# Decoder layer on one core: the second norm's factors issued right behind the first norm's power on GpSimd, and the output bias added by VectorE in one operation per batch

## The chip, the core and the metric

The kernel runs on one core of a Trainium2 chip. A core has TensorE (PE in the profile, its weight loads PEld), VectorE (DVE), ScalarE (ACT), GpSimd (POOL) and SyncE (SP, which here only issues transfers). Each engine takes its instructions strictly in the order in which the program lists them. An instruction that waits for another engine holds up everything behind it in its own queue. The metric is the time on the device in microseconds for one execution, lower is better; several executions are timed and the median counts. One execution is also recorded by the profiler.

## The reference

One decoder layer in float32, on x of shape 16 x 256 x 256 (batch, token, width) and a context of 16 x 77 x 256. Three sublayers, each added to its input and followed by a norm without weights:

```
x = layernorm(x + recurrence(x))            # linear, causal convolution of 4, silu, 16 states scanned over tokens, linear
x = layernorm(x + cross_attention(ctx, x))  # 8 heads of 128
x = layernorm(x + experts(x))               # 8 experts, the best 2 of each token, a capacity of 512 tokens per expert

cross_attention:
  xn = layernorm(ctx) * gamma_media + beta_media
  ln = layernorm(x) * gamma_lat + beta_lat       # x has just been normed: it is normed a second time
  q = ln @ Wq + bq;   k, v = split(concat(xn, ln) @ Wkv + bkv)
  out = softmax(q k^T / sqrt(128)) v @ Wo + bo   # bo is the output's bias
```

The second norm of x in the cross attention needs no new statistics. If the first norm had variance v and factor r = (v + eps)^-0.5, the normed rows have mean 0 and variance v r^2, so the second factor is (v r^2 + eps)^-0.5.

## The kernel before, in words

The kernel goes through the 16 batches one after the other. The main part is one loop over 128 pairs of batch b and head h. For every head it issues keys and queries (`head_kq`, lines 609 and 614), scores and softmax (`head_softmax`, 624 to 634), the turned probabilities (`head_turn`, 646 to 649) and, two heads later, the product with the values (`head_out`, 660). A head costs TensorE some 6 us. Between the heads, lists called `steps`, `mid_steps` and `late_steps` put all other work at fixed places (b, h): the recurrence of later batches, the preparation of batch b+1, and the output projection, norm, routing and result of batch b-1.

The program is written as this sequence, and a scheduler then lists each engine's instructions by when it expects their inputs to be ready. So the order on an engine is not just the order of the source. `tc.issue_after(i)` keeps an instruction behind another one.

The places that matter here:

- `rec_out(nb)` norms the recurrence's result for batch nb. Statistics on VectorE (144 to 147), the power v^-0.5 on GpSimd (`ra`, line 136), and the normed rows `xs` on VectorE (151). It keeps the power's instruction as `normed[nb]`, and ends with the load of x for batch nb+2 (SP). For even nb it stands at head 1 of batch nb-1, for odd nb at head 3 of batch nb-2.
- `prep_norm(nb)` forms the factors of the second norm with `again`: `uz`, `u2z`, `u3z` and the power `rlz`, four small GpSimd operations in a chain (159, 161, 163, 136), and multiplies `xs` by them on VectorE into `zl` (522). For even nb it stands at head 2 of batch nb-1; for odd nb at head 0 of batch nb-1, about five heads after `rec_out`. TensorE then turns `zl` (534), VectorE writes `kvt` (536), and all keys, queries and values of batch nb come from that.
- `project_sums` and `project_pairs` (725 to 770) are the output projection of batch b-1 at heads 1 to 3 of batch b, in a form with fewer products: VectorE makes sums `osum` and differences `ot` of the heads' outputs in place (725, 726, then 729, 730), and TensorE multiplies them in two parts (750). The second part needs line 729.
- In part 0, `project_pairs` also makes `xb` = `xs` + bias on GpSimd, two operations of 128 x 256 per batch (743), issued after `normed[b + 2]` of the batch b that is projected. This holds for batches 0 to 13; batches 14 and 15 go through `project` and `norm_half` (692, 781). `xb` has one buffer, so the next batch's `xb` can be written only when line 151 has read the last one.
- `scatter_second` sends the second batch of a routed pair to the experts' rows in HBM: four indirect transfers issued by GpSimd (990), at head 1 of odd batches, also after `normed`.
- `settle(b)` forms the factors of the third norm's input in the same way (`uo` to `rlo`) and writes the result rows `o` on GpSimd (807).

Of the kernel before, what the change touches and what calls it, by code (L numbers as in the profile page):

```python
# [13 lines left out]
ALU = mybir.AluOpType  # L14
# [4 lines left out]
P = 128  # L19
B, S, D = 16, 256, 256  # L20
# [18 lines left out]
def decoder_layer(  # L39
# [29 lines left out]
    V, A, G, T = nc.vector, nc.scalar, nc.gpsimd, nc.tensor  # L69
# [14 lines left out]
    def bank(name, tag="mm", bufs=2):  # L84
        return ps.tile([P, 512], F32, tag=tag, bufs=bufs, name=name)
# [48 lines left out]
    def rsqrt(v, n, rows, name):  # L134
        r = small.tile([P, n], F32, tag="r", name=f"r{name}")
        powers.append(G.tensor_tensor(r[:rows], v[:rows], nhalf[:rows, 0:n], ALU.pow))
        return r

    def layernorm(dst, src, n, rows, name, behind=None):

        mv = small.tile([P, n, 2], F32, tag="mv", name=f"mv{name}")
        for i in range(n):
            st = small.tile([P, 6], F32, tag="st", name=f"st{name}_{i}")
            V.bn_stats(st[:rows], src[:rows, i, :])
            V.bn_aggr(mv[:rows, i, :], st[:rows])
        v = small.tile([P, n], F32, tag="v", name=f"v{name}")
        V.tensor_scalar(v[:rows], mv[:rows, :, 1], EPS, None, ALU.add)
        r = rsqrt(v, n, rows, name)
        for i in range(n):
            with tc.issue_after(behind.ins) if behind is not None else nullcontext():  # L150
                V.tensor_scalar(
                    dst[:rows, i, 0:D], src[:rows, i, :], mv[:rows, i, 0:1], r[:rows, i : i + 1], ALU.subtract, ALU.mult
                )
        return mv, r

    def again(mv, r, name):

        u = small.tile([P, 2], F32, tag="u", name=f"u{name}")
        G.tensor_tensor(u, mv[:, :, 1], r, ALU.mult)
        u2 = small.tile([P, 2], F32, tag="u2", name=f"u2{name}")  # L160
        G.tensor_tensor(u2, u, r, ALU.mult)
        u3 = small.tile([P, 2], F32, tag="u3", name=f"u3{name}")
        G.tensor_scalar(u3, u2, EPS, 1.0, ALU.add, ALU.mult)
        return rsqrt(u3, 2, P, f"l{name}")
# [15 lines left out]
    bo_s = wpool.tile([P, D], F32, tag="bo", name="bo_s")  # L180
# [24 lines left out]
    def load_x(b):  # L205
        xts[b] = aw.tile([P, 2, D], F32, tag="xt", bufs=3, name=f"xt{b}")
        nc.sync.dma_start(xts[b], x_in[b * S : (b + 1) * S, :].rearrange("(i p) d -> p i d", p=P))
# [116 lines left out]
    sums, yss, xs, stats = {}, {}, {}, {}  # L324
# [90 lines left out]
        for b, r in zip(members, rows):  # L415
            yss[b] = ys[r, :], outw[r, :]

    ysums, normed = {}, {}

    def rec_add(b, n):  # L420

# [12 lines left out]
    def rec_out(b):  # L434

        xs[b] = xpool.tile([P, 2, DX], F32, tag="xs", name=f"xs{b}")
        stats[b] = layernorm(xs[b], ysums.pop(b), 2, P, f"a{b}")
        normed[b] = powers[-1]
        if b + 2 < B:
            load_x(b + 2)  # L440
# [70 lines left out]

    def prep_norm(b):

        r2 = again(*stats.pop(b), f"z{b}")
        zl = b1.tile([P, 2, D], F32, tag="zl", name=f"zl{b}")
        for i in range(2):
            if turned is None:
                V.tensor_scalar(zl[:, i, :], xs[b][:, i, 0:D], r2[:, i : i + 1], None, ALU.mult)
                continue

            with tc.issue_after(turned.ins):
                V.tensor_scalar(zl[:, i, :], xs[b][:, i, 0:D], r2[:, i : i + 1], None, ALU.mult)
        zs[b] = zl
# [193 lines left out]
    def out_block(b, e, i):  # L717
        return outs_t[b].rearrange("p (g e) s -> p g e s", e=2)[:, :, e, i * P : (i + 1) * P]
# [13 lines left out]
    def project_pairs(b, part):  # L732


        x = lambda e, i: out_block(b, e, i)
        w = wo_block
        t = lambda i: wosum[:, i, :, :]
        if part == 0:
            pws[b] = bank(f"pw{b}")
            xbs[b] = xb = b1.tile([P, 2, D], F32, tag="xb", name=f"xb{b}")  # L740
            with tc.issue_after(normed[b + 2].ins):
                for j in range(2):
                    G.tensor_tensor(xb[:, j, :], xs[b][:, j, 0:D], bo_s, ALU.add)
            products = (0, x(0, 0), w(0, 0)), (1, osums[b], t(0)), (2, x(0, 1), w(0, 1))
        else:
            products = (3, x(0, 0), t(1)), (0, x(1, 0), w(1, 0)), (1, osums[b], w(1, 1)), (2, x(1, 1), t(2))
        p = pws[b]
        for r, lhsT, rhs in products:
            for g in range(H // 2):
                T.matmul(  # L750
                    p[:, r * P : (r + 1) * P],
                    lhsT=lhsT[:, g, :],
                    rhs=rhs[:, g, :],
                    start=(part == 0 and r == 0 and g == 0),
                    stop=(g == H // 2 - 1),
                    skip_group_check=True,
                )
        xb = xbs[b]
        y = xb.rearrange("p i d -> p (i d)")
        if part == 0:  # L760
            parts[b] = u = b1.tile([P, 3, P], F32, tag="u", name=f"u{b}")
            A.copy(u.rearrange("p r d -> p (r d)"), p[:, 0 : 3 * P])
            for r in (1, 2):
                V.tensor_tensor(y[:, 3 * P :], y[:, 3 * P :], u[:, r, :], ALU.add)
            return
        u = parts.pop(b)
        V.tensor_tensor(u[:, 0, :], u[:, 0, :], p[:, 3 * P :], ALU.add)
        V.tensor_tensor(y[:, 0 : 3 * P], y[:, 0 : 3 * P], p[:, 0 : 3 * P], ALU.add)
        y3 = y[:, P:].rearrange("p (r d) -> p r d", d=P)
        V.tensor_tensor(y3, y3, u[:, 0:1, :].broadcast_to([P, 3, P]), ALU.add)  # L770
        norms[b] = layernorm(xs[b], xb, 2, P, f"b{b}")
# [249 lines left out]
    for b in range(B):  # L1021
        nb = b + 1
        new_pair = nb % PB == 0 and nb < B
        if b > 0:
            early = 2 * int(b == B - 1)
            if b < B - 1:
                behind(b, 1, project_sums, b - 1, 0)
                at(b, 2, project_pairs, b - 1, 0)
                behind(b, 2, project_sums, b - 1, 1)
                at(b, 3, project_pairs, b - 1, 1)  # L1030
            else:
                at(b, 0, project_last)
                at(b, 2, project, b - 1, 0)
                at(b, 2, project, b - 1, 1)
            at(b, 5 - early, turn_tokens, b - 1)
            if b == B - 1:
                at(b, 6 - early, score_experts, b - 1)
                at(b, 6 - early, choose, b - 1, 1)
                at(b, 7 - early, dispatch, b - 1, 1)
            elif b % 2 == 0:  # L1040
                at(b, 6, score_pair, b - 2)
                behind(b, 6, turn_logits, b - 2)
                behind(b, 6, choose, b - 2, 2)
                behind(b, 7, dispatch, b - 2, 2)
            if b % 2 == 1 and 2 < b < B - 1:
                behind(b, 1, scatter_second, b - 3)
            at(b, 7, settle, b - 1)
        if new_pair:
# [3 lines left out]
            elif nb % 4 == 0:  # L1052
                at(b, 0, rec_state, nb, nb + 3)
                amid(b, 0, rec_scan, nb)
            at(b, 1, rec_add, nb, PB)
            at(b, 1, rec_out, nb)
            at(b, 2, prep_norm, nb)
            at(b, 3, rec_out, nb + 1)
            at(b, 3, prep_keys, nb)
            at(b, 3, prep_sums, nb)  # L1060
# [3 lines left out]
        elif b == 0:  # L1064
            for h in range(2):
                at(0, h, rec_in, 0, 2 * h, 1)
                at(0, h, rec_in, 0, 2 * h + 1, 1)
            at(0, 2, load_xT, 1)
            at(0, 2, rec_state, 1, 1)
            amid(0, 2, rec_scan, 1)  # L1070
            at(0, 3, rec_add, 1, 1)
            at(0, 3, rec_out, 1)
            at(0, 4, prep_norm, 1)
            at(0, 4, prep_keys, 1)
            at(0, 4, prep_sums, 1)
            for n, h in enumerate((5, 6, 7)):
                at(0, h, prep_values, 1, n, False)
                behind(0, h, prep_values, 1, n, True)
            for h in range(NCT - FIRST_CTX):
                behind(0, h, context, FIRST_CTX + h, False)  # L1080
        elif nb < B:
            at(b, 0, prep_norm, nb)
            at(b, 0, prep_keys, nb)
            at(b, 0, prep_sums, nb)
            for n, h in enumerate((1, 4, 6)):
                at(b, h, prep_values, nb, n, False)
                behind(b, h, prep_values, nb, n, True)
# [378 lines left out]
```

## Time and profile before

| what | value |
|---|---|
| time, median of 3 runs | 1169.77 us (1169.11 to 1172.89) |
| the profiled execution's own time | 1171.0 us |
| its span, first to last instruction | 1169.3 us |
| granted TensorE clock | 0.997 |
| busy PE / PEld / DVE / ACT / POOL | 97% / 70% / 67% / 43% / 27% |
| GpSimd, line 743 (`xb`) | 28 operations, 19.2 us |
| GpSimd, line 990 (scatters) | 64 transfers, 66.1 us |
| GpSimd, lines 159 to 163 and 136 for `rlz` | 16 times four operations, 22.0 us |

The share of an engine's busy time is an average over the whole span. The heads run from about 55 us to 1020 us; before that lie the first norms and loads, after it the experts. A matmul's end is modelled, so the lost time of TensorE is best read from the distance of starts: four `pq` matmuls in a row are normally followed by the next group 0.86 to 0.87 us after their first start, and eight `pw` matmuls 0.89 us after. What a wait costs is what lies above that.

### The profile page before, as it was taken

What the parts mean: (1) busy time and instruction counts of PE and PEld (TensorE: products, weight loads), DVE (VectorE), ACT (ScalarE), POOL (GpSimd) and SP (SyncE); (2) the same over time, 40 slices, a digit from 0 to 9 for tenths busy, and PEclk for the clock granted to TensorE, in tenths of its full rate; (3) what the DMA queues carried; (4) which work ended last, traced back from release to release, by engine and by line L of the source; (5) the groups of instructions that cost most, each with busy time, mean ns of one, the idle gap of its engine ahead of it and who ended that gap; (6) DMA issues with size and microseconds to landing.
All of it is one profiled execution on the core that took longest, in us unless ns stands there. A gap on an engine that the chain in (4) does not pass through costs nothing. (4 is left out here: it accounts for less than half of the span.)

```text
span 1169.3 us, 16020 instructions
## 1 busy us (share of the span) xinstructions
PE 1135.1 (97%) x5380; PEld 821.0 (70%) x5380; DVE 782.1 (67%) x2144; ACT 499.0 (43%) x1315; POOL 316.1 (27%) x565
## 2 busy tenths in 40 slices
PE   7999999999999999999999999999999999999996
PEld 3465676767787777677777777777777778876664
DVE  6655877676657776777567757865567555665666
ACT  3344444453444344444444444444444444523331
POOL 2201241114210530242015302340142014144455
PEclk9999999999999999999999999999999999999998
DMA  8741010001000110010000100000001000046652
GB/s 276 206 128 39 20 38 18 11 28 58 19 12 10 54 36 12 28 40 19 12 10 27 37 11 10 18 19 12 10 17 46 20 10 15 21 159 138 181 160 90
DMA packets 47417, 60.63 MB, mean 52 GB/s; under 512 B 7957, under 2 KB 37374, under 8 KB 47336
## 3 DMA queue, kind: packets, MB, share of 16 engines
q1 hardware_dynamic: 39686, 50.18, 14.1%
q0 software_dynamic: 6048, 9.22, 3.3%
q8 instruction: 42, 0.69, 0.2%
q10 hardware_dynamic: 1602, 0.23, 0.1%
q14 instruction: 39, 0.32, 0.1%
HBM read 36.33 MB, written 30.78 MB: 57 GB/s over the span
## 5 line engine op out<-in xcount | busy, mean ns | idle before, releaser
L660 PE MATMUL po<-ptt,v 128*128 128x256 f32 (+1 forms) x768 | 189.2, 381 | 1.6 <-DVE rs L632 1.6
L660 PEld LDWEIGHTS po<-ptt,v 128*128 128x128 f32 (+1 forms) x768 | 142.0, 190 | 51.7 <-issue 34.4
L609 PE MATMUL pk<-kvt,wkv_s 128*128 128x333 f32 x512 | 165.4, 444 | 0.0
L624 PE MATMUL s<-kt,qt 128*128 128x333 f32 x512 | 164.5, 443 | 0.0
L626 DVE TENSOR_REDUCE nm<-s 128x2 f32<-128x666 f32 x128 | 108.3, 846 | 72.1 <-PE s L624 68.1
L630 ACT ACTIVATE p<-s,nm 128x333 f32<-128x333 f32 x256 | 135.7, 536 | 44.5 <-DVE nm L626 44.2
L614 PE MATMUL pq<-kvt,wq_s 128*128 128x256 f32 x512 | 131.2, 378 | 0.0
L609 PEld LDWEIGHTS pk<-kvt,wkv_s 128*128 128x128 f32 x512 | 91.1, 191 | 45.6 <-issue 22.9
L668 ACT ACTIVATE ot<-po,bkv_s 128x256 f32<-128x256 f32 x128 | 60.9, 476 | 140.3 <-PE po L660 135.7
L624 PEld LDWEIGHTS s<-kt,qt 128*128 128x128 f32 x512 | 96.3, 188 | 31.6 <-issue 1.3
L614 PEld LDWEIGHTS pq<-kvt,wq_s 128*128 128x128 f32 x512 | 96.7, 189 | 30.8 <-issue 1.0
L649 ACT COPY ptt<-pb 77x256 f32<-77x256 f32 x128 | 47.3, 369 | 164.1 <-PE pb L646 161.0
L634 DVE TENSOR_SCALAR p<-p,rs 128x333 f32<-128x333 f32 x256 | 98.5, 421 | 3.3
L990 POOL DMA_INDIRECT xg<-xs,sidx x64 | 66.1, 1032 | 98.3 <-ACT ot L668 38.9
L648 DVE COPY ptt<-pa 128x512 f32<-128x512 f32 x128 | 87.3, 682 | 0.7 <-PE pa L646 0.7
L646 PEld LDWEIGHTS pa<-ident,p 128*128 128x128 f32 x512 | 63.9, 141 | 29.3
L611 ACT ACTIVATE kt<-pk,bkv_s 128x333 f32<-128x333 f32 x128 | 69.1, 540 | 28.2 <-PE pk L609 21.7
L646 PE MATMUL pa<-ident,p 128*128 128x128 f32 x512 | 76.8, 273 | 0.0
L351 DVE SCALAR_TENSOR_TENSOR cv<-hp,cw,cv 128x512 f32<-128x512 f32 (+1 forms) x108 | 74.1, 692 | 1.6
L616 ACT ACTIVATE qt<-pq,bqs 128x256 f32<-128x256 f32 x128 | 61.1, 478 | 20.2 <-PE pq L614 15.3
L336 PE MATMUL ph<-xT,inw 128*128 128x512 f32 (+1 forms) x144 | 63.1, 567 | 5.5 <-DMA inw<-in_in_wT 4.4
L1275 PE MATMUL pf<-w,it 128*128 128x256 f32 x272 | 61.3, 381 | 2.0 <-ACT ye L1285 1.7
(264 smaller groups left out, 1764.6 us busy)
## 6 DMA issues: line engine op xcount, KB each, us to landing
v<-vc SPq DMA_DIRECT2D x16, 308.0 KB
xg<-zero SPq DMA_DIRECT2D x34, 131.0 KB
xe<-xg SPq DMA_DIRECT2D x8, 524.0 KB
xt<-in_x_in SPq DMA_DIRECT2D x16, 256.0 KB
out<-o SPq DMA_DIRECT2D x16, 256.0 KB
w<-in_w1T SPq DMA_DIRECT2D x8, 512.0 KB
w<-in_w2T SPq DMA_DIRECT2D x8, 512.0 KB
oe<-ye SPq DMA_DIRECT2D x15, 256.0 KB
```

Source lines behind the costliest of these rows:

```text
L351: conv = V.scalar_tensor_tensor(cv, hp[:, :, k : k + S], cw[:, c, k : k + 1], cv, ALU.mult, ALU.add)
L609: T.matmul(pk[:, 0:J], lhsT=wkv_s[:, k, f], rhs=kvt[:, k, :], start=(k == 0), stop=(k == DC - 1))
L611: A.activation(kt, pk[:, 0:J], AF.Identity, bias=bkv_s[:, h : h + 1])
L614: T.matmul(pq[:, 0:S], lhsT=wq_s[:, k, f], rhs=kvt[:, k, 0:S], start=(k == 0), stop=(k == DC - 1))
L624: T.matmul(s[:, ic, 0:J], lhsT=qt[:, ic * P : (ic + 1) * P], rhs=kt, start=True, stop=True)
L626: V.tensor_reduce(nm, s[:, :, 0:J], AX.X, ALU.max, negate=True)
L630: A.activation(p[:, ic, :], s[:, ic, 0:J], AF.Exp, bias=nm[:, ic : ic + 1], accum_out=sm[:, ic : ic + 1])
L634: V.tensor_scalar(p[:, ic, :], p[:, ic, :], rs[:, ic : ic + 1], None, ALU.mult)
L646: T.transpose(dst[0:jn, c0 : c0 + P], pn[:, ic, j0 : j0 + jn], ident)
L648: turned = V.tensor_copy(ptt[:, 0:2, :], pt01.rearrange("p (j i) -> p j i", j=2))
L660: T.matmul(po[:, 0:S], lhsT=vs[b][0:jn, jc, h * DH : (h + 1) * DH], rhs=ptt[0:jn, jc, :], start=(jc == 0), stop=(jc == 2),)
L990: dma = G.indirect_dma_start(out=xg[:, :], out_offset=bass.IndirectOffsetOnAxis(ap=sidx[:, t, c : c + 1], axis=0), in_=xs[b + t // GT][:, ...
```

## The change

The factors of the second norm are formed in `rec_out`, right behind the norm's power, and kept in `factors` until `prep_norm` fetches them. The power that `normed` names becomes the last power issued, which is now `rlz` and no longer `ra`: what is issued after `normed` is issued behind the factors too. The bias is added to `xs` by one VectorE operation of 128 x 512 per batch, with the bias row read twice through a broadcast, and without `issue_after`.

```
-    ysums, normed = {}, {}
+    ysums, normed, factors = {}, {}, {}
 ...
         xs[b] = xpool.tile([P, 2, DX], F32, tag="xs", name=f"xs{b}")
         stats[b] = layernorm(xs[b], ysums.pop(b), 2, P, f"a{b}")
+
+        factors[b] = again(*stats[b], f"z{b}")
         normed[b] = powers[-1]
         if b + 2 < B:
             load_x(b + 2)
 ...
     def prep_norm(b):
 
-        r2 = again(*stats.pop(b), f"z{b}")
+        r2 = factors.pop(b)
         zl = b1.tile([P, 2, D], F32, tag="zl", name=f"zl{b}")
 ...
             xbs[b] = xb = b1.tile([P, 2, D], F32, tag="xb", name=f"xb{b}")
-            with tc.issue_after(normed[b + 2].ins):
-                for j in range(2):
-                    G.tensor_tensor(xb[:, j, :], xs[b][:, j, 0:D], bo_s, ALU.add)
+            V.tensor_tensor(xb, xs[b][:, :, 0:D], bo_s.unsqueeze(1).broadcast_to([P, 2, D]), ALU.add)
```

## The prediction, before the result was known

> **What bounds the kernel now.** I read the totals first, then the waits of TensorE and of VectorE, then the order of time around the longest of them.
>
> ```profile
> PE 1135.1 (97%) x5380; PEld 821.0 (70%) x5380; DVE 782.1 (67%) x2144; ACT 499.0 (43%) x1315; POOL 316.1 (27%) x565
> PE pw L750 <- DVE ot L729: 3.5, 6, 1.3
> ...
> DVE zl L522 <- POOL rlz L136: 31.7, 6, 5.3
> ```
>
> TensorE is the bound: of 1169.3 us only 34 are idle, and much of that lies in the first 55 us and in the experts' stage after 1020. So VectorE's 31.7 us of waiting for `rlz` are not 31.7 us to be had. They count only where TensorE ends up waiting: six times for `ot`, line 729, which stands behind `zl` on VectorE. One of the six in the order of time, GpSimd, then VectorE, then TensorE (start, length, operation; in brackets the idle time before and what ended it):
>
> ```profile
> 393.16 0.72 POOL L136 TENSOR_TENSOR ra<-va,nhalf 128x2 f32<-128x2 f32 x1 [0.67 <-DVE va L147]
> 394.07 1.18 POOL L990 DMA_INDIRECT xg<-xs,sidx  x1 [0.19 <-issue]
> ...
> 399.27 1.33 POOL L743 TENSOR_TENSOR xb<-xs,bo_s 128x256 f32<-128x256 f32 x2
> 400.55 0.20 POOL L159 TENSOR_TENSOR uz<-mva,ra 128x2 f32<-128x2 f32 x1
> ...
> 401.39 0.72 POOL L136 TENSOR_TENSOR rlz<-u3z,nhalf 128x2 f32<-128x2 f32 x1
> ```
>
> ```profile
> 395.96 0.90 DVE L634 TENSOR_SCALAR p<-p,rs 128x333 f32<-128x333 f32 x2
> 402.14 0.61 DVE L522 TENSOR_SCALAR zl<-xs,rlz 128x256 f32<-128x256 f32 x2 [5.29 <-POOL rlz L136]
> 402.68 0.68 DVE L729 TENSOR_TENSOR ot<-osum,ot 128x512 f32<-128x512 f32 x1
> ```
>
> ```profile
> 401.10 1.02 PE L614 MATMUL pq<-kvt,wq_s 128*128 128x256 f32 x4
> 403.41 1.16 PE L750 MATMUL pw<-wosum,ot 128*128 128x128 f32 x8 [1.29 <-DVE ot L729]
> ```
>
> `ra` ends at 393.88. Four scatters and two `xb` stand between it and the four small operations that end in `rlz` at 402.11. VectorE waits 5.29 us, TensorE loses 403.41 - 401.10 - 0.86 (the usual distance) = 1.45 us, and 0.11 more in the first group after the gap (1.00 us to the next start, normally 0.89).
>
> **The change part by part.** I set the built order of the changed kernel against the old one. TensorE's order is the same, so its time changes only by its waits.
>
> 1. *`rlz` ahead of the scatters and without `xb` between (batches 4, 6, 8, 10, 12, 14).* From 393.88 four operations at the pace of 400.55 to 402.11 take 1.56 us, so `rlz` is ready at 395.5, perhaps 1 us later beside VectorE. The new VectorE order has half of `zl` ahead of `p` and half behind; `p` starts at 395.96 anyhow. `ot` of line 729 then ends near 398.5, and TensorE wants it at 401.96. All six waits go: 3.5 us idle, and with the modelled ends (1.56 lost against 1.29 idle) 0.27 more each: 3.5 + 6 x 0.27 = 5.1 us. Gain 5.1. It cannot be a loss here: 3.4 us are left. What is late next is line 726 at the same places (TensorE's wait for it, 0.6 us at 395.90), which stands ahead of all this and stays. The scatters move back by 1.6 us; their rows are first read after 1010 us, so 0. On GpSimd only `tsum`, first needed at 408, stands behind them; 395.5 + 4 x 1.3 = 400.7, so 0.
>
> 2. *`xb` off GpSimd.* It frees 28 x 0.70 = 19.2 us there, which bounds nothing. But VectorE is slowed beside it: two `xs` take 1.46 us beside `xb`, against 0.74 elsewhere.
>
> ```profile
> 143.34 1.46 DVE L151 TENSOR_SCALAR xs<-xt,mva,ra 128x256 f32<-128x256 f32 x2 [0.83 <-POOL ra L136]
> ...
> 166.40 1.30 DVE L151 TENSOR_SCALAR xs<-xt,mva,ra 128x256 f32<-128x256 f32 x2 [0.60 <-POOL ra L136]
> ...
> 170.90 1.53 PE L660 MATMUL po<-ptt,v 128*128 128x256 f32 x6 [1.63 <-DVE rs L632]
> ```
>
> Behind the first, in an unbroken VectorE row, line 726 keeps TensorE idle for 0.69 us at 149.98; 0.72 earlier it does so hardly at all: gain 0.7. Behind the second come `cv` (1.12 instead of 0.75), `nm`, `cv` and the copy `ptt`, for which TensorE waits 1.63 us at 170.90: 0.56 + 0.37 = 0.9 us earlier. Gain together 1.6; below, 0 if the small GpSimd operations now beside them slow them as much. In later odd stages (413.62, 1.30 us) TensorE does not wait, so 0.
>
> 3. *`xb` on VectorE, 14 operations.* The nearest row is the sum of two SBUF tensors of the same shape in line 726: 0.68 us, 0.61 from start to start. Built places: batch 0 right before a 1.64 us wait for ScalarE (116.97), free. Odd batches (413) behind `rs`: the 0.56 that `xs` no longer loses pays for it. Batches 4, 8, 12 (350) behind `rs`: `p` would end at 352.6 and is wanted at 354.32, free. Left are batches 2, 6 and 10. There the new order has `xb` and one more `cv` ahead of `nm` and `ptt`:
>
> ```profile
> 471.40 0.75 DVE L351 SCALAR_TENSOR_TENSOR cv<-hp,cw,cv 128x512 f32<-128x512 f32 x1
> 472.06 0.85 DVE L626 TENSOR_REDUCE nm<-s 128x2 f32<-128x666 f32 x1
> 472.82 0.75 DVE L351 SCALAR_TENSOR_TENSOR cv<-hp,cw,cv 128x512 f32<-128x512 f32 x1
> 473.48 0.69 DVE L648 COPY ptt<-pa 128x512 f32<-128x512 f32 x1
> ...
> 474.80 1.46 PE L660 MATMUL po<-ptt,v 128*128 128x256 f32 x6
> ```
>
> `ptt` ends at 474.17; 0.61 (`xb`) and 0.66 (`cv`) later is 475.44, and TensorE wants it at 474.80: it waits 0.7 us. ScalarE's order changes there too (`kt` ahead of the exponentials, `qt` behind the tanh); `qt` is then ready near 476.5, and the scores that need it have moved to 476.8, so no second wait. Cost 3 x 0.7 = 2.1. Bounds: 0 if the scheduler's order costs nothing after all, 3 x (0.7 + 0.86) = 4.7 if each `xb` is slowed as `osum` is once (1.54 us at 391.46 beside GpSimd's `sums`, 0.68 without). I take 2.1, since at 472 GpSimd has only a power of two elements at work, beside which `cv` and `osum` at 146 us kept their 0.7.
>
> The Trainium skill speaks against this part: "SBUF — State Buffer", section "Who interferes with whom", says that a VectorE sum with both inputs in SBUF contends with a GpSimd operation that reads SBUF, the later one being blocked for the whole instruction. By that rule `osum` at 391.46 waits for `sums`, which ends at 392.45, and the trace agrees. For the three places the rule would make it the 4.7 above if GpSimd were ahead, 2.1 if not.
>
> 4. *Moves with one answer.* In batch 0 `rc8` now stands behind `u3z` and `rlz` (0.28 + 0.75 later); `ctx` needs it and TensorE waits there already (88.97): about 0.2 us lost. On SP the load of x for batch nb+2 goes ahead of a result's store and `w1` of expert 0 ahead of another; each is ready at about the same time as what it passes, 0. In odd batches the third norm's factors stand behind `rlz` instead of between two `xb`, same length, 0.
>
> Sum: -5.1 - 1.6 + 2.1 + 0.2 = **-4.4 us**. The profiled execution, 1171.0 us (span 1169.3 and 1.7 around it), would take 1166.6. It is 1.2 above the median, so for the median 1169.77 - 4.4 = **1165.4 us**, 0.38% faster.
>
> **The rivals.**
>
> *A, `xb` costs nothing on TensorE.* If at batches 2, 6, 10 the copy still comes in time: -6.5, 1163.3 us. For it: 10 of 14 places hide it. Against: 0.63 us of room for 1.27.
>
> *B, the shared reading of SBUF.* Each of the three places costs 1.56, and the small GpSimd chain takes half of the 1.6 back: -5.1 - 0.8 + 4.7 + 0.2 = -1.0, 1168.8 us. For it: `osum` at 391.46. Against: GpSimd is nearly idle at these places.
>
> *C, nothing moves.* TensorE's wait for line 729 stays under another releaser, for instance `p`, whose exponential is late. Then -1.6 + 2.1 + 0.2 = +0.7, 1170.5 us. Against: 3.4 us of room.
>
> *D, slower: VectorE's added work passes to TensorE at all 14 places.* Its place is between `rs` and `p`, its price 0.61 to 1.47 each. At 0.61 it is 8.5 + 0.2 - 6.7 = +2.0, 1171.8 us; blocked, at 1.47, it is 20.6 + 0.2 - 6.7 = +14.1, 1183.9 us. It is slower by over 0.3% from (6.5 + 3.5) / 14 = 0.71 each. For it: VectorE waits only 1 to 2 us per head. Against: the room counted in step 3.
>
> **How the numbers follow.** About 0.3% (3.5 us) is what a measurement can tell from no change; the three runs lie 3.8 us apart. Chances: the forecast 0.50, A 0.14, B 0.20, C 0.07, D 0.09 (within 0.3% at its lower price 0.02, slower 0.07). The forecast lies only 0.9 us beyond the bound, so of its 0.50 I count 0.43 as faster and 0.07 as within. Faster: 0.43 + 0.14 = 0.57. Within: 0.07 + 0.20 + 0.07 + 0.02 = 0.36. Slower: 0.07. The range goes from A less 0.8 for the spread, 1162.5, to B, rounded up, 1169.2; it leaves out C, D and a little of the ends, some 0.2.
>
> **What would show it.** Right: VectorE's wait for `rlz` falls from 31.7 us to under 5, TensorE's wait for line 729 to near 0; `xb` is a VectorE row of 14 at about 0.69 us; three new waits of TensorE before `po` for `ptt`, half a microsecond each, near 234, 474 and 714; GpSimd is 19 us less busy. Wrong: `xb` at over 1 us (B), waits for `ptt` or `p` in odd batches too (D), waits for 729 left (C).

## The result, and the profile after

| | kernel before | changed kernel |
|---|---|---|
| median, 12 executions each | 1171.57 us (1169.11 to 1173.54) | 1168.02 us (1164.15 to 1169.99) |
| profiled execution, own time | 1171.0 us | 1169.99 us |
| its span | 1169.3 us | 1168.3 us |
| heads, first `pk` to first `pe` | 967.94 us | 964.29 us |

The ratio is 0.9968 with a 95% interval of 0.9959 to 0.9977: 3.7 us faster, between 2.7 and 4.8. The kernel before, measured beside it, took 1171.57 us over 12 executions, where the first three had given 1169.77; against that new base the forecast of -4.4 us reads 1167.2. The forecast time itself, 1165.4, was missed by 2.6 us, of which 1.8 are the base. By the bare time of 1168.0 rival B's 1168.8 lies nearer than the forecast, so the ratio and the traces have to tell the two apart. The 3.7 us are also only just more than the 3.5 that the prediction set as the bound to no change.

The totals and the longest waits of TensorE and VectorE in the changed kernel (the lines of the source have moved by two, so the old 729 is now 731):

```profile
PE 1135.5 (97%) x5380; PEld 821.7 (70%) x5380; DVE 784.2 (67%) x2158; ACT 499.1 (43%) x1315; POOL 300.6 (26%) x537
PE po L662 <- DVE rs L634: 2.6, 4, 0.7
PE px L373 <- DMA xpw<-in_xp_wT: 2.0, 1, 2.0
...
PE pw L750 <- DVE ot L728: 1.2, 2, 0.6
```

```profile
DVE nm L628 <- PE s L626: 72.7, 55, 2.0
DVE u L767 <- PE pw L750: 41.4, 14, 3.2
```

VectorE's 31.7 us of waiting for `rlz` are gone altogether. More than half of them have turned into waits for TensorE's products (`u` behind `pw`, 22.4 us before and 41.4 now), which hold up nothing on TensorE. TensorE's six waits for line 729 are gone, and four waits before `po` stand in the list, three of them new.

The place that the prediction showed around 400 us, in the changed kernel, in the order of time on GpSimd, VectorE and TensorE:

```profile
393.86 0.72 POOL L136 TENSOR_TENSOR ra<-va,nhalf 128x2 f32<-128x2 f32 x1 [0.66 <-DVE va L147]
394.66 0.19 POOL L159 TENSOR_TENSOR uz<-mva,ra 128x2 f32<-128x2 f32 x1
...
395.49 0.69 POOL L136 TENSOR_TENSOR rlz<-u3z,nhalf 128x2 f32<-128x2 f32 x1
396.35 1.12 POOL L990 DMA_INDIRECT xg<-xs,sidx  x1 [0.17 <-issue]
```

```profile
396.54 0.34 DVE L524 TENSOR_SCALAR zl<-xs,rlz 128x256 f32<-128x256 f32 x1
396.79 0.84 DVE L636 TENSOR_SCALAR p<-p,rs 128x333 f32<-128x333 f32 x2
397.55 0.33 DVE L524 TENSOR_SCALAR zl<-xs,rlz 128x256 f32<-128x256 f32 x1
397.80 0.70 DVE L731 TENSOR_TENSOR ot<-osum,ot 128x512 f32<-128x512 f32 x1
```

```profile
401.80 1.02 PE L616 MATMUL pq<-kvt,wq_s 128*128 128x256 f32 x4
402.67 1.05 PE L750 MATMUL pw<-wosum,ot 128*128 128x128 f32 x8
```

`rlz` ends at 396.18, 1.6 us behind `ra`, with the scatters behind it. `ot` ends at 398.50 and is wanted at 402.67, so 4.2 us of room have taken the place of a wait of 1.29. The distance from `pq` to `pw` is the usual 0.87 us.

The price of the change, around 472 us (VectorE, then TensorE):

```profile
471.20 0.69 DVE L743 TENSOR_TENSOR xb<-xs,bo_s 128x512 f32<-128x512 f32 x1
471.81 0.75 DVE L351 SCALAR_TENSOR_TENSOR cv<-hp,cw,cv 128x512 f32<-128x512 f32 x1
472.47 0.85 DVE L628 TENSOR_REDUCE nm<-s 128x2 f32<-128x666 f32 x1
473.23 0.79 DVE L351 SCALAR_TENSOR_TENSOR cv<-hp,cw,cv 128x512 f32<-128x512 f32 x1
473.94 0.68 DVE L650 COPY ptt<-pa 128x512 f32<-128x512 f32 x1
```

```profile
473.09 1.02 PE L576 MATMUL pv<-wsum,tsum 128*128 128x512 f32 x2
474.77 1.53 PE L662 MATMUL po<-ptt,v 128*128 128x256 f32 x6 [0.66 <-DVE rs L634]
```

`xb` and one more `cv` stand ahead of the copy `ptt`, which ends at 474.62; `po` starts 0.15 us later. (The profile names `rs`, which is ready at about the same time. `po` reads `ptt`, and with the bias added twice, below, where `rs` starts only 1 us after `po`, the profile names `ptt` for the same wait of 0.66 us.)

TensorE runs the same 5380 matmuls in the same order in both kernels, so one can take, for each matmul, its start after minus its start before. Where that difference steps, time was won or lost. All steps between 50 and 1010 us, each with the refill of up to 0.1 us behind it:

| place in the trace of before | step, us | what it is |
|---|---|---|
| 89 | +0.12 | `ctx` in batch 0, later by `rc8` |
| 150 | -0.72 | line 726, whose `xs` is no longer slowed |
| 171 | -0.95 | `ptt` behind a slowed `xs` and `cv` |
| 234, 475, 715 | +0.81, +0.82, +0.82, and 0.075 behind each | `ptt` behind `xb`, batches 2, 6, 10 |
| 286, 403, 526, 644, 767, 878 | -0.46, -1.56, -0.44, -1.55, -0.46, -0.67 | the six waits for line 729 |
| sum | -4.0 | |

(The heads of the table above are 3.65 us shorter, not 4.0, because the first `pe`, which ends that stretch, waits for a transfer and loses 0.34 us; in a second recorded execution of the changed kernel it does not, and the heads take 963.82 us, 4.12 less than before.)

The last stage, the experts, shifts by up to 2 us either way from one recorded execution to the next (steps of -1.8 to +1.6 us between 1075 and 1130 us in the pairs of traces compared here), and so does the start. The terms are therefore read from the heads, where the second recorded execution of the changed kernel gave every one of these steps again within 0.01 us.

### The profile page after: what moved, and what is told of

Read it like the earlier page. It is cut to its first block, busy times and chain, and to the rows that moved or that the text cites. A ratio compares the mean times of both kernels' runs of the same rounds, so it can differ in the third digit from the quotient of the medians.

```text
span 1168.3 us, 16011 instructions
## 1 busy us (share of the span) xinstructions
PE 1135.5 (97%) x5380; PEld 821.7 (70%) x5380; DVE 784.2 (67%) x2158; ACT 499.1 (43%) x1315; POOL 300.6 (26%) x537
## 4 chain that ended last, share of the span: by engine, by line
PE 80%; DVE 12%; DMA 3%; issue 2%; POOL 2%; ACT 1%; POOLq 0%; ACTq 0%; DVEq 0%
PE po L662 12%; PE s L626 10%; PE pk L611 10%; PE pq L616 8%; PE pv L576 7%; PE pw L750 7%; PE pi L1248 4%; PE pf L1275 4%; PE pa L648 4%; PE ph L336 3%; DVE cv L351 2%; PE pvc L494 2%; PE pb L648 2%; PE pw L680 1%; DVE nm L628 1%
```

## The experiments

All kernels of the first four experiments were timed beside the kernel before at 1170.63 us (1167.23 to 1174.48, 17 executions), those behind them at 1171.41 us (1169.28 to 1173.0, 16 executions).

### Only the factors moved

```
-            V.tensor_tensor(xb, xs[b][:, :, 0:D], bo_s.unsqueeze(1).broadcast_to([P, 2, D]), ALU.add)
+            with tc.issue_after(normed[b + 2].ins):
+                for j in range(2):
+                    G.tensor_tensor(xb[:, j, :], xs[b][:, j, 0:D], bo_s, ALU.add)
```

(against the changed kernel)

> One part alone: the factors right behind the norm's power, the bias still added by GpSimd in two operations behind the factors. My theory: the six waits of VectorE for rlz go as in the changed kernel, TensorE gets its 5.1 us back, and nothing is added on VectorE, so no new waits of 0.8 us in batches 2, 6 and 10; the two waits near 150 and 171 us (0.9 and 1.9 us of TensorE) stay, because GpSimd still adds the bias beside VectorE. Sum -5.1 + 0.1 = -5.0 us, 1166.6 us, ratio 0.957 to 0.997 of a percent apart from the changed kernel at most: 0.9957 against 0.9968. VectorE will wait some 3.5 us for xb behind the scatters, six times, at no cost to TensorE. Rival: that wait takes the place of the old one, TensorE keeps a wait of 0.5 to 1.5 us in the same six stages, and the time stays within 1 us of before.

Measured: 1165.54 us median (1164.57 to 1166.27), ratio 0.9958 (0.9941 to 0.9975). The sum with the bias is late here, as `rlz` was before, but nobody on TensorE stands behind it. VectorE's waits, and its place at 400 us:

```profile
DVE xb L766 <- POOL xb L745: 21.0, 6, 3.5
```

```profile
398.00 0.70 DVE L731 TENSOR_TENSOR ot<-osum,ot 128x512 f32<-128x512 f32 x1
...
403.00 0.62 DVE L766 TENSOR_TENSOR xb<-xb,u 128x128 f32<-128x128 f32 x2 [3.51 <-POOL xb L745]
```

VectorE waits 21 us in six places, and `ot` is 4 us early all the same. Against the kernel before, TensorE's starts step by -5.13 at the six places, -0.43 at 171 and +0.19 at 150, and not at all at 234, 475 and 715; with the +0.12 at 89, -5.3 in the heads. The +0.19 was not expected: GpSimd's `xb`, now behind the factors, stands beside `osum` there, which takes 1.22 us. By the traces, then, the factors alone win more than the whole change, and the bias on VectorE costs 1.3 us on top of them (-4.0 against -5.3). The times alone don't tell the two kernels apart: the intervals of their ratios overlap.

### Only the bias moved

```
-        factors[b] = again(*stats[b], f"z{b}")
 ...
-        r2 = factors.pop(b)
+        r2 = again(*stats.pop(b), f"z{b}")
```

> The other part alone: the bias on VectorE, the factors still formed late, behind the four scatters. My theory: rlz comes 1.3 us earlier than before but still 5 us behind the power; in the built order half of zl now stands ahead of p, so p waits for rlz and TensorE waits for p before its transposes: about 1.4 us in batches 3, 7, 11, 2.5 us in 5 and 9, 1.6 us in 13, together 10.8. Sum 10.8 - 5.1 - 1.6 + 2.4 = +6.5 us, 1178 us, slower than before. Rival: it was the two bias operations on GpSimd that made rlz late enough to hurt TensorE; then this part alone brings the gain, some -4 us, 1167.5 us.

Measured: 1177.73 us (1177.01 to 1180.11), ratio 1.0063 (1.0045 to 1.0081): slower, by 7 us. TensorE's and VectorE's waits, and the place on VectorE and TensorE:

```profile
PE pa L646 <- DVE p L634: 8.5, 6, 2.1
```

```profile
DVE zl L522 <- POOL rlz L136: 29.7, 6, 5.0
```

```profile
399.95 0.35 DVE L522 TENSOR_SCALAR zl<-xs,rlz 128x256 f32<-128x256 f32 x1 [4.96 <-POOL rlz L136]
400.22 0.69 DVE L634 TENSOR_SCALAR p<-p,rs 128x333 f32<-128x333 f32 x2
...
400.67 1.20 PE L646 MATMUL pa<-ident,p 128*128 128x128 f32 x4 [2.11 <-DVE p L634]
```

`rlz` is earlier only by the two `xb` that stood ahead of it, 1.3 us; the four scatters still do. But VectorE's new order has one `zl` ahead of `p`; presumably the scheduler, without the two `xb` in its reckoning, thinks `rlz` earlier than it is. The wait of 5 us, which was hidden behind `p`, now stands ahead of it, and `p` is wanted at once. The second part of the change is a loss without the first, and at these places it is the order, not VectorE's added 0.6 us, that costs. The six waits, 8.5 us idle by the modelled ends, cost TensorE's starts 9.5 us and 1.5 more in the first groups behind them; behind two of them a further 1.5 and 1.7 us are lost, which was not expected and is taken up below.

### The bias behind the copy in three batches

```
-            V.tensor_tensor(xb, ...)
+            with tc.issue_after(turned.ins) if b in (2, 6, 10) else nullcontext():
+                V.tensor_tensor(xb, ...)
```

> The changed kernel, with the bias of batches 2, 6 and 10 added later: behind the copy of the turned probabilities one batch on, where VectorE now waits for TensorE. My theory: the three new waits of TensorE for ptt (0.8 us each) go and nothing comes in their place, since p at the new place has over 2 us of room: 2.4 us less than the changed kernel, 1165.6 us for 1168.0, ratio 0.9947 of before. Rival: a VectorE operation of 0.6 us costs TensorE wherever it stands between rs and p; then the three waits move to batches 3, 7 and 11 and the time stays at 1168.

Measured: 1164.16 us (1162.34 to 1166.49), ratio 0.9949 (0.9931 to 0.9967), the lowest median of all. TensorE's starts step by -0.81, -0.82 and -0.82 against the changed kernel, at 235, 475 and 714 and nowhere else in the heads:

```profile
469.85 0.68 DVE L650 COPY ptt<-pa 128x512 f32<-128x512 f32 x1
470.45 0.74 DVE L351 SCALAR_TENSOR_TENSOR cv<-hp,cw,cv 128x512 f32<-128x512 f32 x1
```

```profile
470.31 1.02 PE L576 MATMUL pv<-wsum,tsum 128*128 128x512 f32 x2
471.17 1.46 PE L662 MATMUL po<-ptt,v 128*128 128x256 f32 x6
```

With `ptt` ready at 470.53, `po` follows `pv` after 0.86 us without a wait. The heads are 6.8 us shorter than before the change (6.8 = 4.0 + 2.8, from the two comparisons of starts). The interval of its ratio still overlaps that of the changed kernel and that of the factors alone; it is the trace that shows the three waits gone and nothing new in their place. The `cv` that stood ahead of the copy together with `xb` is behind it again too, as it was before the change, so this run does not part the share of `xb` from that of `cv`.

### GpSimd's sums put back beside VectorE's

```
             V.tensor_tensor(xb, ...)
+            spare = b1.tile([P, D], F32, tag="spare", name=f"spare{b}")
+            with tc.issue_after(normed[b + 2].ins):
+                for j in range(2):
+                    G.tensor_tensor(spare, xs[b][:, j, 0:D], bo_s, ALU.add)
```

> The changed kernel with GpSimd's two bias operations per batch put back at their place behind normed, their sum written to a spare buffer that nobody reads; the other engines' orders are those of the changed kernel. My theory: GpSimd has time for them, and what they cost is what they do to VectorE beside them: osum near 147 us is held up by about 1.2 us and TensorE waits 0.8 to 1 us for line 728 near 151 us again; near 171 us nothing, since they now stand later; in the stages from batch 3 on no new wait of TensorE. Together about +1 us over the changed kernel, 1169 us. Rival: the two operations beside VectorE cost nothing and the gains near 150 and 171 us came from the order; then no wait near 151 us and the time of the changed kernel.

Measured: 1167.11 us (1166.35 to 1168.95), ratio 0.9974 (0.996 to 0.9987): by the times no different from the changed kernel. The comparison of starts is sharper: +0.91 at 150 and +0.52 at 171, and nothing else over 0.08 us in the heads. VectorE and GpSimd ahead of the first:

```profile
144.69 1.22 DVE L727 TENSOR_TENSOR osum<-ot 128x512 f32<-128x512 f32 x1
145.83 1.12 DVE L351 SCALAR_TENSOR_TENSOR cv<-hp,cw,cv 128x512 f32<-128x512 f32 x1
...
144.52 1.89 POOL L747 TENSOR_TENSOR spare<-xs,bo_s 128x256 f32<-128x256 f32 x2
```

In the changed kernel these two take 0.68 and 0.75. The other engines' orders are the same, so the slowing beside GpSimd's sums is shown as the cause of the 0.9 us at 150. The 0.52 at 171 was not expected. There one `cv` takes 1.26 us beside `spare` (0.74 without) and delays `ptt`, and in the kernel with only the factors moved the same row takes 1.26 beside `xb`, which leaves the same 0.52 to be gained:

```profile
168.11 1.26 DVE L351 SCALAR_TENSOR_TENSOR cv<-hp,cw,cv 128x512 f32<-128x512 f32 x1
```

So once the factors are moved, which brings 0.43 at 171, taking `xb` off GpSimd brings 0.52 more. That split holds for this order alone. With only the bias moved the same place gains 0.90 us already, and `xs` and `cv`, 1.30 and 1.12 us before, are back at their usual times:

```profile
164.50 0.77 DVE L151 TENSOR_SCALAR xs<-xt,mva,ra 128x256 f32<-128x256 f32 x2 [0.60 <-POOL ra L136]
165.19 0.74 DVE L351 SCALAR_TENSOR_TENSOR cv<-hp,cw,cv 128x512 f32<-128x512 f32 x1
```

Taking `xb` off GpSimd is enough by itself there; moving the factors only lets `xb` slow a later `cv` instead of these two.

### The bias added twice on VectorE

```
             V.tensor_tensor(xb, ...)
+            V.tensor_tensor(xb, ...)
```

> The sum with the bias is computed a second time into the same tile, so VectorE has 14 more sums of 128 x 512, 0.61 us each from start to start, and the result is the same. TensorE's, ScalarE's and GpSimd's orders stay; on VectorE the second sum stands behind p, rs or ptt, and in batches 2, 6 and 10 behind ptt, so not ahead of the copy that TensorE waits for there. Theory (VectorE's work costs only where TensorE waits for it): 0.0 to 1.0 us over the changed kernel, ratio to the kernel before 0.9965 to 0.998, and no new wait for p of more than 0.3 us. Rival D (VectorE's added work passes to TensorE at all 14 places): 14 x 0.61 = 8.5 us over it, ratio 1.004.

Measured: 1168.84 us (1167.54 to 1170.8), ratio 0.9982 (0.9972 to 0.9992); the changed kernel beside it took 1167.22 us, ratio 0.9968. That is 1.6 us more by the medians, whose intervals overlap, and 2.3 in the heads of the traces, where at most 1.0 was expected, and far from the 8.5 of rival D. The comparison of starts puts most of it in four places: 0.77 at 176, and 0.46 to 0.48 each at 236, 476 and 716. Another 0.2 lies at 389 and 397, where no added sum stands; why is open. The other ten sums cost nothing where they stand. VectorE and GpSimd at the first place and at one of the three:

```profile
172.50 1.63 DVE L744 TENSOR_TENSOR xb<-xs,bo_s 128x512 f32<-128x512 f32 x1
...
172.29 1.28 POOL L359 TENSOR_TENSOR sums<-hs 128x512 f32<-128x512 f32 x1
```

```profile
476.71 1.31 DVE L636 TENSOR_SCALAR p<-p,rs 128x333 f32<-128x333 f32 x2
...
476.21 1.29 POOL L359 TENSOR_TENSOR sums<-hs 128x512 f32<-128x512 f32 x1 [2.42 <-DVE rs L634]
```

The doubled sum moved VectorE's next operations under GpSimd's `sums`. `xb` took 1.63 us and ended 0.56 behind the end of `sums`, `p` took 1.31 instead of 0.69. So a blocked sum, the upper bound of the prediction's step 3, does exist; it takes 0.95 us more here, where the bound had 0.86. The changed kernel avoids it at all 14 places by where they stand, not by its kind of instruction.

### The changed kernel once more

No edit.

> The changed kernel as it is, timed once more beside the doubled bias. Its terms in the trace come to -4.0 us against the kernel before and its measured ratio was 0.9968: 1166.4 to 1167.4 us if the kernel before takes 1170.6, ratio 0.996 to 0.9975. If the start (the wait for the recurrence's small weights and the half clock behind it, 1.8 us in the profiled run of the changed kernel) belongs to the change, it is there again; if it differs from execution to execution, it need not be.

Measured: 1167.22 us (1166.18 to 1170.02), ratio 0.9968 (0.9955 to 0.9981). Its start had no wait for the weights `xpw` of 2 us, though the half clock was there again; the steps of the heads came out the same.

### A longer chain ahead of the late `zl`

Two further operations of two elements that add 0 and multiply by 1, in the chain of `rlz`, on top of the kernel with only the bias moved; and then three:

```
         G.tensor_scalar(u3, u2, EPS, 1.0, ALU.add, ALU.mult)
+        for k in range(extra):
+            u4 = small.tile([P, 2], F32, tag=f"u4{k}", name=f"u4{k}{name}")
+            G.tensor_scalar(u4, u3, 0.0, 1.0, ALU.add, ALU.mult)
+            u3 = u4
```

> The bias alone on VectorE, with two more operations of two elements in the chain of the second norm's factors of batches 4, 6, 8, 10, 12 and 14 (they add 0 and multiply by 1), 0.28 us each. All other engines keep their order. TensorE's six waits for p grow from 1.0, 2.1, 1.0, 2.1, 1.0 and 1.2 us to about 1.6, 2.7, 1.6, 2.7, 1.6 and 1.8. If a granted clock of 0.5 follows a wait by its length, and the bound lies at 2 us, it comes behind the same two waits as before and the time grows by 6 x 0.56 = 3.4 us over that of the bias alone, to 1181. If the bound lies at 1.5, it comes behind all six: 4 x 1.7 us more, 1188. If it has nothing to do with the wait, the two places change.

Measured: 1182.4 us (two executions, 1180.42 and 1184.38), ratio 1.0094 (1.0065 to 1.0124). TensorE's six waits are 1.55, 2.65, 1.56, 2.65, 1.53 and 1.76 us, as expected. The half clock follows the fourth only, though the second is as long. The time is 1.4 us above the 1181 of a bound at 2 us.

> As with two more operations, but three: the six waits of TensorE for p grow to about 1.85, 2.95, 1.85, 2.95, 1.85 and 2.1 us. By a bound of 2 us the half clock comes behind the second, the fourth and now the sixth: 5.0 + 1.7 us over the bias alone, 1184.5. By a bound between 1.8 and 1.85 all six, 1190. If it has nothing to do with the wait's length, the places don't follow it.

Measured: 1184.58 us (1184.09 and 1185.07), ratio 1.0113 (1.009 to 1.0136). The six waits are 1.83, 2.93, 1.85, 2.93, 1.83 and 2.06 us, and the half clock follows the second only, not the fourth of the same length and not the sixth. The time fits a bound on the wait's length, but by chance: the places do not, so that theory falls. What holds instead is in the last section.

## Why the prediction was right, and where its sizes were off

- **Step 1, the six waits, -5.1.** Measured -5.13 in the changed kernel and again with the factors alone. `rlz` was ready 1.6 us behind `ra`, as its row said, and nothing was late next at these places. The first part alone does it. With the bias alone the waits for line 729 go too, but VectorE still waits 29.7 us for `rlz`, and TensorE waits for `p` instead.
- **Step 2, `xb` off GpSimd, -1.6.** Measured -0.72 and -0.95, together -1.67, and the reason held as well: with the bias alone, which takes `xb` off GpSimd and leaves the factors late, the same two places gain 0.72 and 0.90. With the factors alone the first place loses 0.19 and the second gains 0.43, so at 171 the two parts of the change overlap and their gains don't add up. The half of this step that rival B let the small operations take back was not taken: both `xs` take 0.74 us beside them.
- **Step 3, `xb` ahead of `ptt`, +2.1.** The places were right, three of fourteen; the size was not. This is the term that was mis-sized: 3 x (0.82 + 0.075) = 2.7 instead of 3 x 0.7 = 2.1. The prediction compared the end of `ptt` with the start that TensorE wanted, 475.44 - 474.80 = 0.64, rounded up. But `po` starts 0.15 us after `ptt` ends (474.62 to 474.77), the second `cv` took 0.79 instead of 0.75, and the first group behind a gap takes 0.075 us more; all three were left out here, though step 1 had counted the last for its own waits. The step was also wrong that GpSimd has only a power of two elements at work there: two `o` of 128 x 256 run beside `nm` and that second `cv` (line 807, at 472.55 in the changed kernel). Nor is it the sum alone that costs: by the step's own numbers `xb` takes 0.61 us and there were 0.63 of room, or 0.48 less the 0.15 just named, so without the `cv` that came ahead with it the wait would have been some 0.1 us (an estimate; no run shows it).
- **Step 4, +0.2.** Measured +0.12. It is there with the factors alone and not with the bias alone, as the step has it.
- **The sum.** -4.4 was forecast, the steps come to -4.0, the times to -3.7 (-4.8 to -2.7). The 0.3 between the last two is inside the interval, and no step in the heads stands behind it. Nearly all of the 0.4 between the first two is step 3. Luck had a part in the range: the base moved by 1.8 us, which no step foresaw, and the measured time stayed 1.2 us below its upper end.
- **The rivals.** A (`xb` free) is not what happened, but its -6.5 is what the chip gives once `xb` stands behind the copy: -6.8. B's blocked sum does not occur in the changed kernel (all 14 `xb` take 0.67 to 0.69 us) and occurs in the doubled one. C falls, no wait for line 729 is left. D falls: in the changed kernel eleven of the 14 `xb` cost TensorE nothing, and 14 more sums cost 2.3 us, not 8.5.
- **What would show it.** GpSimd became 15.5 us less busy, not 19: `rlz` and `rlo` now stand beside other VectorE work and take 0.91 and 0.88 us in the mean, 0.73 and 0.77 before. Nothing waits for that. The new waits were 0.66 us long where half a microsecond was expected.

## What to carry to other kernels

A wait on one engine is worth what stands behind it in that engine's queue: 31.7 us of waiting for `rlz` were worth 5.1, 21 us of waiting for `xb` were worth nothing, and 29.7 us cost 9.5 as soon as one operation that TensorE needs stood behind them. When work is moved to an engine with room, count the room at each place up to the start of the waiting operation, not up to the end of the one that it waits for, and put the work behind what the bound engine needs next: the sum, with the `cv` that came along, costs 0.9 us ahead of the copy and nothing behind it. A change in two parts should be tried part by part, since here one part won 5.3 us, the other cost 1.3 on top of it by the traces, and alone it cost 7.

## What the runs showed of the hardware

**The granted clock fell by windows, not by waits.** Where the bias alone was moved, TensorE's clock was granted at 0.5 for 3.41 us after two of its six waits, at 400.65 and 646.41 us. These starts lie 245.76 us apart, 72.0 times 3.413, and wherever another trace here has more than one drop, the one behind the last matmul of each included, they too lie whole multiples of 3.413 us apart. So the record falls into windows of 3.413 us that run through from start to end. What the windows show, granted clock third from the end, first with the bias alone, then with the chain longer by three:

```profile
643.00:646.41 3.41, 1.30 (x8) 0.61 (x7) 1.42 (x5) 0.00 (x0) 1.70 (x5) 1.00 0.02 6
646.41:649.82 3.41, 3.41 (x10) 2.39 (x9) 2.94 (x6) 1.26 (x4) 0.00 (x0) 0.50 0.00 0
```

```profile
645.63:649.04 3.41, 1.58 (x7) 0.81 (x5) 0.00 (x0) 0.48 (x1) 2.59 (x9) 1.00 0.04 10
649.04:652.45 3.41, 2.31 (x12) 1.76 (x13) 2.89 (x8) 0.37 (x1) 0.35 (x1) 1.00 0.00 0
```

The first number behind the comma is TensorE's busy time. A wait of 2.11 us that lay whole in one window left it 1.30 us busy, and the next window ran at half the clock. A wait of 2.93 us that a window's edge cut into 1.83 and 1.10 left 1.58 us, and nothing followed. In the heads of all ten traces the windows with 2.10, 2.11, 2.57 and 2.65 us idle were followed by the half clock, and none with 1.83 or less was. The half clock cost 1.3 to 1.7 us each time. The windows are not tied to the program: they begin at another time in each trace, and of the two waits of 2.65 us in one execution, with the chain longer by two, only one was followed by the half clock. So a wait of 2.1 us can meet this in one execution and not in another, which would make it a source of scatter, and one recorded execution does not tell its mean price.

The Trainium skill, "TensorE: Matmul & The Clock Gate", section "What's actually happening", describes such a free-running window of 3413 ns, and the traces agree. It names an idle window as what brings the half clock; here about 2.1 of the 3.4 us were enough.

**The start of the program meets the same windows.** In the profiled execution of the changed kernel `px` waited 2.0 us for the weights `xpw`, and the clock was granted at 0.5 from 14.66 to 18.07 us. In the second recorded execution the clock fell there without the wait, in the kernel with the bias added twice there was the wait and no fall, and in the one with the bias behind the copy there was neither. So both come and go with the execution. Whether the change makes them more frequent is open: the wait for `xpw` is in three of the six recorded executions of kernels with the factors moved and in none of the four others, too few to tell. One window at the start, the one up to 14.16 us with the chain longer by three, was followed by the half clock with only 1.7 us idle by the modelled ends, and one with as much idle time, with the bias added twice, was not; why is left open.

**VectorE beside GpSimd.** A sum on VectorE that met a GpSimd operation of 128 x 512 ended 0.56 us after that one, about as if it had started then (172.50 above). Beside a power of two elements it went otherwise (changed kernel, GpSimd and VectorE):

```profile
146.16 0.88 POOL L136 TENSOR_TENSOR rlz<-u3z,nhalf 128x2 f32<-128x2 f32 x1
```

```profile
146.52 0.75 DVE L351 SCALAR_TENSOR_TENSOR cv<-hp,cw,cv 128x512 f32<-128x512 f32 x1
```

`cv` started while the power ran and kept its usual 0.75 us; it is the power that took 0.88 instead of 0.69. The Trainium skill, "SBUF — State Buffer", section "Who interferes with whom", has the later of the two blocked for the whole instruction. The sum beside `sums` agrees with it; `cv` beside the power does not.
